# Conditioned attention on one core: a new order of the columns, with x, residual and output moved for pairs of steps, and all weights turned by VectorE

## The chip, the cores and the metric

The kernel runs on one core of one Trainium2 chip. The metric is device time in microseconds; lower is better. A change of the time is told from no change by runs of both kernels on the same chip.

## The reference

x is (8, 512, 512) in float32: 8 batches of 512 tokens of 512 columns. There are 16 heads of 32 columns.

```python
Q = split_heads(x @ Wq.T + bq);  K = split_heads(x @ Wk.T + bk);  V = split_heads(x @ Wv.T + bv)
tQ = split_heads(tokens @ Wq.T + bq);  tK = split_heads(tokens @ Wk.T + bk)   # one token per batch
cQ = Q + tQ;  cK = K + tK
scores = einsum('bhqd,bhkd->bhqk', cQ, cK) / sqrt(32)
attn = softmax(scores, axis=-1)
out = einsum('bhqk,bhkd->bhqd', attn, V)
x = x + out.transpose(0, 2, 1, 3).reshape(B, S, 512)
```

All is float32, and the weights are dense 512 x 512 matrices. The condition (`tokens`, 8 x 512) adds the same vector to each query and key of a batch.

## The kernel before

The work is cut into T = 32 steps: 8 batches times G = 4 groups of 4 heads. A step t holds the four heads of group t % 4 of batch t // 4, one head on each quarter of the 128 partitions. The order of the instructions on TensorE, VectorE, ScalarE and GpSimd is that in which the Python code records them; SyncE's transfers are put in an order by the framework, by when their operands are ready.

*Two kinds of steps.* The exponentials of a softmax must lie with the keys on the partitions for the product with V, but the row maxima are found with the queries there. Odd steps (`BLOCKED`) compute the scores once (`row_max`, L592; `row_scores`, L619), take the row maxima on VectorE (L588 and L630), and write the exponentials (`denominators`, L653) into the first eight rooms of `arena`. From there they are turned: SyncE moves blocks of 32 rows between partition quarters (`exchange`, L643, in two halves of 16 transfers of 128 KB), and VectorE turns each 32 x 32 block in place (`turn_blocks`, L636, eight turnings of 128 x 1024 for each odd step). Even steps compute the scores twice: once with the queries on the partitions, for the maxima and sums (their exponentials go back into PSUM), and once with the keys there (`exponentials`, L718), with the maxima brought in by a small matmul of `maxT` (L723). `maxT` is made by GpSimd (`split_max`, L675) and a transposing transfer on SyncE (`turn_max`, L692). These exponentials go to `arena` from room 8 on, eight rooms in a step, wrapping at `ROOMS`.

*The loop* runs over t = 1 to 28. Each step has four items:

- V: `weighted(t - 1)`, the product of step t - 1's exponentials with V (`times_v`, L739), then reciprocal, transpose, scaling, residual (`send`, L807),
- q, k, v: the projections of a later group, in the seven-product form of a 2 x 2 block product; four products in one step, three in the next (`four_products` L511, `three_products` L533).

Each item also holds the scores and maxima of one quarter of the queries of step t + 1 (or of t + 2, in the last item), their exponentials, and, in even steps, one quarter of `exponentials(t, i)`. The eight PSUM banks go round: `begin` (L133) deals four of them to the scores of an item. Which turnings follow which item is a table (`TURNED`, L1028: with u the odd step whose blocks are turned, (-1, 2) is the k item of step u - 1, and (0, 3) the v item of step u). Which transfers are recorded behind which item is a table too (`ORDERS`, L1040).

*The single buffer of blocks.* `room` (L222) has one buffer, so the exchange of the next odd step starts when `weighted` of the last one has read it, in the V item of the even step.

*Columns.* Group g is columns 128 g to 128 g + 127. `spread` (L161) gives 32 columns of every 32nd token, so that a transfer of x, of the residual (`load_residual`, L180) or of the output (`store`, L817) writes 32 partitions in 512 runs of 128 bytes, and four transfers make a step's tile; VectorE's block transpose (L373, L810) then turns it.

*The start* (L247 to L950). Wq by rows in four transfers, x of batch 0 and the first rows of Wk by rows, turned by TensorE and copied out of PSUM; the rest of Wk, and Wv, in runs of 128 bytes, turned by VectorE (`turn_w`, L900). `condition` and `condition_end` (L836, L844) compute the projected tokens. GpSimd makes the sums of weight blocks for the seven-product form (`combine_w`, L332; four sums for each weight).

Of the kernel before, what the change touches and what calls it, by code (L numbers as in the profile page):

```python
# [17 lines left out]
def kernel(  # L18
# [52 lines left out]
    ROOMS = 14  # L71
# [4 lines left out]
    xp = ctx.enter_context(tc.tile_pool(name="xp", bufs=2))  # L76
# [73 lines left out]
    xs = {}  # L150

    def load_x(n, queue=nc.sync):

        if n < B * NS:
            xs[n] = early[:, 3 + n, :]
            queue.dma_start(xs[n], x[n // NS, n % NS * P : (n % NS + 1) * P, :])

# [3 lines left out]
    def spread(a, d):  # L161

        return a.rearrange("(f j) d -> j f d", j=BL)[:, :, d : d + BL]

    def load_block(n):

        b, cc = divmod(n, NC)
        if b < B:
            xs[n] = xp.tile([P, NB, BL], F32, tag="x", name=f"x_{n}")
            for h in range(HG):  # L170
                nc.sync.dma_start(xs[n][h * BL : (h + 1) * BL], spread(x[b], cc * P + h * BL))

    xr = {}
    late = []
# [5 lines left out]
    def load_residual(t):  # L180

        b, g = divmod(t, G)
        if turned_by_vector(t):
            if late:
                xr[t] = late_part(t % 2 * 10 + 2).rearrange("p (f e) -> p f e", e=BL)
            else:
                xr[t] = op.tile([P, NB, BL], F32, tag="xr", name=f"xr_{t}", bufs=1)
            for h in range(HG):
                nc.sync.dma_start(
                    xr[t][h * BL : (h + 1) * BL], spread(x[b], g * P + h * BL)  # L190
                )
        else:

            xr[t] = xT[b][:, g, :]
# [32 lines left out]
    for n in ("q", "k", "v"):  # L227
        ws[n] = stage.tile([P, NC, D], F32, tag="w", name=f"w_{n}")

    def load_w(n, w, queue, cs=range(NC)):  # L230
        wv = w.rearrange("(c p) d -> p c d", p=P)
        for c in cs:
            queue.dma_start(ws[n][:, c, :], wv[:, c, :])
# [12 lines left out]

    load_w("q", Wq, nc.sync, [0])  # L247
    load_x(0, nc.scalar)
    load_x(1)
    wk0 = early[:, 7, :]  # L250
    nc.scalar.dma_start(wk0, Wk[:P, :])

    cond_sb = early[: B + 2, 0, :]
    nc.sync.dma_start(cond_sb[:B, :], cond)
    nc.sync.dma_start(cond_sb[B : B + 1, :], bq.rearrange("(o d) -> o d", o=1))
    nc.sync.dma_start(cond_sb[B + 1 : B + 2, :], bk.rearrange("(o d) -> o d", o=1))
    load_x(2)
    load_x(3, nc.scalar)
    load_w("q", Wq, nc.sync, [1])
    onesb = const.tile([P, P], BF16, tag="onesb", name="onesb")  # L260
    nc.vector.memset(onesb, 1.0)
    ones = const.tile([P, P], F32, tag="ones", name="ones")
    nc.vector.memset(ones, 1.0)
    table = const.tile([P, 1], F32, tag="table", name="table")
    nc.scalar.activation(table, ones[:, :1], AF.Exp)
    load_w("q", Wq, nc.sync, [2, 3])

    for n, w, f in (("k", Wk, HG), ("v", Wv, 0)):
        wn = ws[n].rearrange("p c (f e) -> p c f e", e=BL)
        for cc in range(NC):  # L270
            for h in range(HG):
                nc.sync.dma_start(
                    wn[h * BL : (h + 1) * BL, cc, f:], spread(w, cc * P + h * BL)[:, f:]
                )
    bvl = const.tile([P, 1], F32, tag="bvl", name="bvl")
    nc.sync.dma_start(bvl, bv.rearrange("(g p o) -> g p o", g=G, o=1)[G - 1])
    bvs = const.tile([P, G, BL], F32, tag="bvs", name="bvs")
    for h in range(HG):
        nc.sync.dma_start(
            bvs[h * BL : (h + 1) * BL],  # L280
            bv.rearrange("(o g h e) -> o h g e", o=1, g=G, h=HG)[:, h].broadcast_to([BL, G, BL]),
        )

# [14 lines left out]
    condT = const.tile([P, NC, HD], F32, tag="condT", name="condT")  # L298
    nc.vector.memset(condT, 0.0)
# [10 lines left out]
    def transpose_w(n, dc, pt, odd=None, of=None):  # L310

        odd = dc % 2 if odd is None else odd
        of = ws[n][:, dc, :] if of is None else of
        for cc in range(NC):
            nc.tensor.transpose(
                pt[:, cc * P : (cc + 1) * P], of[:, cc * P : (cc + 1) * P], ident
            )
        o = wT[n][:, :, dc * P : (dc + 1) * P]
        pv = pt.rearrange("p (c s) -> p c s", c=NC)
        if n == "q":  # L320
            if odd:
                nc.vector.tensor_scalar(o, pv, SCALE, None, ALU.mult)
            else:
                nc.scalar.activation(o, pv, AF.Copy, scale=SCALE)
        elif odd:
            nc.vector.tensor_copy(o, pv)
        else:
            nc.scalar.copy(o, pv)
# [23 lines left out]
    def transpose_x(n, pt, leaves=nc.vector.tensor_copy):  # L352

        b, sc = divmod(n, NS)
        if b >= B:
            return
        if sc == 0:
            xT[b] = xtp.tile([P, NC, S], F32, tag="xT", name=f"xT_{b}")
        for cc in range(NC):
            nc.tensor.transpose(  # L360
                pt[:, cc * P : (cc + 1) * P], xs[n][:, cc * P : (cc + 1) * P], ident
            )
        leaves(xT[b][:, :, sc * P : (sc + 1) * P], pt.rearrange("p (c s) -> p c s", c=NC))
        if n > 1:
            load_block(n + 2)

    def turn_x(n):
        b, cc = divmod(n, NC)
        if b >= B:
            return  # L370
        if cc == 0:
            xT[b] = xtp.tile([P, NC, S], F32, tag="xT", name=f"xT_{b}")
        nc.vector.transpose(xT[b][:, cc, :], xs[n].rearrange("p f i -> p (f i)"))  # L373
        to_load.append(n + 2)
# [3 lines left out]
    def load_blocks():  # L378
        while to_load:
            load_block(to_load.pop(0))  # L380
# [385 lines left out]
    def masked(t):  # L766
# [3 lines left out]
        apart = op.tile([P, HG, NS, NS], F32, tag="apart", name=f"apart_{t}")  # L770
# [36 lines left out]
    def send(t, y_, rec):  # L807
# [4 lines left out]
        nc.gpsimd.tensor_tensor(y, y, xr.pop(t), ALU.add)  # L812
        to_store.append((t, y))
# [3 lines left out]
    def store():  # L817
        while to_store:
            t, y = to_store.pop(0)
            b, g = divmod(t, G)  # L820
            for h in range(HG):
                nc.sync.dma_start(spread(out[b], g * P + h * BL), y[h * BL : (h + 1) * BL])
# [11 lines left out]
    part = {}  # L834

    def condition(n, pt):  # L836


        for cc in range(NC):
            nc.tensor.matmul(pt[cc * HD : (cc + 1) * HD, :], condT[:, cc, :], wT[n][:, cc, :])  # L840
        part[n] = early[:, 1 + "qk".index(n), :]
        nc.scalar.copy(part[n], pt)

    def condition_end(n, pt, on):  # L844

        i = "qk".index(n)
        untranspose(part[n], pt)
        sum4 = const.tile([P, NC, B], F32, tag=f"sum4{n}", name=f"sum4_{n}")
        nc.vector.tensor_reduce(
            sum4,  # L850
            pt.rearrange("p (d c e) -> p d e c", d=NC, c=NC)[:, :, 0:B, :],
            AX.X,
            ALU.add,
        )
        on.tensor_tensor(
            tok[:, i], sum4, bias2[:, i, :].unsqueeze(2).broadcast_to([P, NC, B]), ALU.add
        )
        on.tensor_tensor(apart_tok[:, i], tok[:, i, 1::2], tok[:, i, 0::2], ALU.subtract)
# [10 lines left out]
    def first_part(n, pt, h):  # L869
        for cc in range(NC):  # L870
            project_qk_part(0, n, cc, pt, slice(h * HS, (h + 1) * HS))

    transpose_w("q", 0, bank(6), 0)
    transpose_x(0, bank(3))
    transpose_x(1, bank(7), nc.scalar.copy)
    transpose_w("k", 0, bank(5), 1, wk0)
    pc = bank(1)
    BB = B + 2
    for cc in range(NC):
        nc.tensor.transpose(  # L880
            pc[:, cc * BB : (cc + 1) * BB], cond_sb[:, cc * P : (cc + 1) * P], ident[:BB, :BB]
        )
    pcv = pc[:, : NC * BB].rearrange("p (c b) -> p c b", b=BB)
    nc.vector.tensor_copy(condT[:, :, 0:B], pcv[:, :, 0:B])
    bias2 = const.tile([P, 2, NC], F32, tag="bias2", name="bias2")
    nc.vector.tensor_scalar(bias2[:, 0, :], pcv[:, :, B], 2.0 * SCALE, None, ALU.mult)
    nc.vector.tensor_scalar(bias2[:, 1, :], pcv[:, :, B + 1], 2.0, None, ALU.mult)
    first_part("q", pq, 0)
    transpose_x(2, bank(0))
    transpose_x(3, bank(3), nc.scalar.copy)  # L890
    first_part("k", pk, 0)
    for half in range(2):
        combine_x(0, half, nc.gpsimd)
    transpose_w("q", 1, bank(7), 1)
    first_part("q", pq, 1)
    transpose_w("q", 2, bank(1), 0)
    transpose_w("q", 3, bank(0), 1)
    first_part("k", pk, 1)

    def turn_w(n, ccs, rows=slice(0, D)):  # L900
        for cc in ccs:
            nc.vector.transpose(wT[n][:, cc, rows], ws[n][:, cc, rows])

# [421 lines left out]
```

## Time and profile before

| | |
|---|---|
| time, median of 3 runs | 712.62 us (711.2 to 715.9) |
| profiled execution: time | 712.44 us |
| profiled execution: span | 710.6 us |
| TensorE busy | 691.2 us (97%) |
| VectorE busy | 571.3 us (80%) |
| ScalarE busy | 544.6 us (77%) |
| GpSimd busy | 280.3 us (39%) |
| mean granted TensorE clock | 0.981 |
| DMA | 90.24 MB, 237273 packets, 221163 of them under 512 bytes |

A row of a view by time has the start, the length, the engine (PE is TensorE, DVE VectorE, ACT ScalarE, POOL GpSimd, SPq the issuing of transfers on SyncE), the line of the code, the operation, output <- input, the shape and a count; in brackets the idle time before it and what ended it. A row of the view by windows has the window and its length, then for PE, PEld (weight loads), DVE, ACT and POOL the busy time and the number of instructions, then the granted TensorE clock, the share of the DMA engines and GB/s. A row of the view by groups has the busy time, the mean length in ns, the idle time before and what ended most of it. A busy TensorE is not one at its peak: matmuls are pipelined, and a matmul that runs at a lower clock is busy for longer.

### The profile page before, as it was taken

How to read it: one execution, taken by the hardware profiler on the slowest of the kernel's cores; microseconds unless marked ns; L12 is line 12 of the kernel's file. 1: busy time of each engine (PE TensorE's matmuls, PEld its weight loads, DVE VectorE, ACT ScalarE, POOL GpSimd, SP SyncE). 2: the span in 40 equal slices, each digit the busy share in tenths (PEclk: the TensorE clock that was granted, in tenths of full speed). 3: DMA queues.
4: the chain of work that ended last, by engine and by line, in shares of the span. 5: the costliest groups of instructions: out<-in, count | busy, mean ns of one | idle time of the engine just before them, and what ended most of it. 6: DMA issues, size and time to landing. Idle time of an engine off the chain costs nothing.

```text
span 710.6 us, 21535 instructions
## 1 busy us (share of the span) xinstructions
PE 691.2 (97%) x8488; PEld 305.1 (43%) x8488; DVE 571.3 (80%) x810; ACT 544.6 (77%) x1399; POOL 280.3 (39%) x330
## 2 busy tenths in 40 slices
PE   9999999999999999999999999898999999999997
PEld 7444443444434444444434444343343444444432
DVE  3797887879688887969879787787878889697777
ACT  2587795978869798797968779687696978879664
POOL 3720532526236161444415254252542526243271
PEclk9999999999999999999999999999899999999999
DMA  6627548476776857677675766857577575663211
GB/s 183 105 39 167 121 108 177 81 157 139 154 153 115 182 94 164 140 152 161 121 160 105 149 142 124 175 97 159 121 141 164 103 168 120 142 150 51 34 31 30
DMA packets 237273, 90.24 MB, mean 127 GB/s; under 512 B 221163, under 2 KB 221675, under 8 KB 237173
## 3 DMA queue, kind: packets, MB, share of 16 engines
q1 hardware_dynamic: 235412, 87.83, 60.8%
q8 instruction: 66, 1.08, 0.7%
q10 hardware_dynamic: 1760, 1.05, 0.5%
q14 instruction: 35, 0.28, 0.1%
HBM read 19.75 MB, written 8.39 MB: 40 GB/s over the span
## 4 chain that ended last, share of the span: by engine, by line
PE 67%; SPq 16%; DMA 5%; DVE 4%; ACT 3%; issue 3%; POOL 0%; DVEq 0%; ACTq 0%; POOLq 0%
PE psum L463 27%; SPq L651 16%; PE psum L746 15%; PE psum L621 15%; PE psum L726 4%; DMA out_dram<-res 2%; PE psum L406 2%; ACT psum L667 2%; PE psum L723 2%; DVE nmax L588 2%; DMA blocks<-arena 1%; DVE blocks L641 1%; DVE nmax L630 1%; ACT arena L667 1%; DMA early<-in_x_dram 1%
## 5 line engine op out<-in xcount | busy, mean ns | idle before, releaser
L667 ACT ACTIVATE psum<-psum,nmax 128x512 f32<-128x512 f32 x256 | 169.0, 662 | 91.1 <-DVE nmax L588 79.8
L588 DVE TENSOR_REDUCE nmax<-psum 128x1 f32<-128x512 f32 x272 | 172.2, 678 | 43.0 <-PE psum L621 42.5
L621 PE MATMUL psum<-kT,qT 32*128 32x512 f32 x1024 | 177.1, 625 | 10.9 <-ACT psum L667 10.9
L641 DVE STREAM_TRANSPOSE blocks<-blocks 128x1024 f32<-128x1024 f32 x112 | 134.5, 1221 | 40.0 <-DMA out_dram<-res 24.8
L737 ACT ACTIVATE arena<-psum 128x512 f32<-128x512 f32 x264 | 136.4, 602 | 33.7 <-PE psum L726 24.5
L667 ACT ACTIVATE arena<-psum,nmax 128x512 f32<-128x512 f32 x224 | 152.8, 697 | 5.3 <-issue 4.9
L630 DVE TENSOR_REDUCE nmax<-psum 128x2 f32<-128x1024 f32 x114 | 138.1, 1212 | 1.1 <-PE psum L621 1.1
L202 POOL TENSOR_TENSOR xr<-xr,bvs 128x512 f32<-128x512 f32 x29 | 37.2, 1283 | 172.7 <-DMA xr<-in_x_dram 172.6
L621 PEld LDWEIGHTS psum<-kT,qT 32*128 32x128 f32 x1024 | 64.0, 183 | 89.5 <-ACT psum L667 33.1
L811 POOL TENSOR_TENSOR res<-res,recs 128x512 f32<-128x512 f32 x30 | 31.5, 1051 | 120.3 <-DVE res L810 111.0
L746 PE MATMUL psum<-arena,v 128*32 128x512 f32 x576 | 77.8, 659 | 0.0
L726 PE MATMUL psum<-qT,kT 32*128 32x512 f32 x528 | 67.9, 587 | 0.0
L746 PE MATMUL psum<-blocks,v 128*32 128x512 f32 x448 | 51.9, 596 | 0.0
L667 ACT ACTIVATION_READ_ACCUMULATOR psum<-psum,nmax 128x1 f32 x256 | 51.8, 202 | 0.0
L463 PE MATMUL psum<-wc_v,xc 128*32 128x256 f32 x768 | 50.6, 381 | 0.0
L463 PE MATMUL psum<-xc,wc_q 128*32 128x256 f32 x720 | 48.3, 387 | 0.0
L667 ACT ACTIVATION_READ_ACCUMULATOR arena<-psum,nmax 128x1 f32 x224 | 47.8, 213 | 0.0
L463 PE MATMUL psum<-xc,wc_k 128*32 128x256 f32 x720 | 47.4, 381 | 0.0
L810 DVE STREAM_TRANSPOSE res<-psum 128x512 f32<-128x512 f32 x28 | 19.5, 697 | 30.0 <-PE psum L746 30.0
L812 POOL TENSOR_TENSOR res<-res,xr 128x512 f32<-128x512 f32 x29 | 37.2, 1283 | 2.3
L463 PE MATMUL psum<-wT_v,xT 128*32 128x256 f32 x512 | 34.3, 382 | 0.2 <-ACT arena L737 0.2
L746 PEld LDWEIGHTS psum<-arena,v 128*32 128x32 f32 x576 | 15.9, 118 | 42.8 <-issue 23.5
(193 smaller groups left out, 894.2 us busy)
## 6 DMA issues: line engine op xcount, KB each, us to landing
blocks<-arena SPq DMA_DIRECT2D x448, 128.0 KB, 2.4
out_dram<-res SPq DMA_DIRECT2D x122, 64.0 KB, 2.1
xr<-in_x_dram SPq DMA_DIRECT2D x116, 64.0 KB, 2.4
x<-in_x_dram SPq DMA_DIRECT2D x112, 64.0 KB, 2.4
w_q<-in_L_cond_Wq_dram SPq DMA_DIRECT2D x4, 256.0 KB, 3.8
w_v<-in_L_cond_Wv_dram SPq DMA_DIRECT2D x16, 64.0 KB, 2.3
w_k<-in_L_cond_Wk_dram SPq DMA_DIRECT2D x16, 48.0 KB, 2.7
early<-in_x_dram ACTq DMA_DIRECT2D x2, 256.0 KB, 3.9
```

The costliest lines, as they stand in the source:

```text
L202: nc.gpsimd.tensor_tensor(xr[t], xr[t], bias, ALU.add)
L463: nc.tensor.matmul(pt[r], still[:, r], moving, start=(kc == kcs[0]), stop=(kc == kcs[-1]))
L588: nc.vector.tensor_reduce(nmax[t][:, qc, j : j + 1, 0], pt, AX.X, ALU.max, negate=True)
L621: nc.tensor.matmul(pt, qkT["q", t][r, qc * P : (qc + 1) * P], qkT["k", t][r, :], start=True, stop=True,)
L630: nc.vector.tensor_reduce(nmax[t][:, qc, pr * 2 : pr * 2 + 2, 0], pt, AX.X, ALU.max, negate=True)
L641: nc.vector.transpose(e, e)
L651: nc.sync.dma_start(to.rearrange("p c h s -> p (c h s)"), of)
L667: nc.scalar.activation(to, of, AF.Exp, bias=nmax[t][:, qc, j, :], accum_out=sums[t][:, qc, j, :],)
L726: nc.tensor.matmul(bank[j], qkT["k", t][r, kc * P : (kc + 1) * P], qkT["q", t][r, :], start=False, stop=True,)
L737: nc.scalar.activation(e[:, i, :], bank[pr * 2 + i], AF.Exp)
L746: nc.tensor.matmul(pt[j * HD : (j + 1) * HD, :], vs[b % 2][:, kc, (g * HG + j) * HD : (g * HG + j + 1) * HD], e, start=(kc == chunks[0]), ...
L812: nc.gpsimd.tensor_tensor(y, y, xr.pop(t), ALU.add)
```

## The change

- *Columns.* Group g now holds columns 32 g to 32 g + 31 of each quarter of the 512. Two steps that follow each other (g and g + 1) then lie side by side, and one transfer takes both in runs of 256 bytes: x (`load_pair`), the residual (`load_residual`, two pairs of buffers, loaded a pair ahead) and the output (`store`, once in a pair; GpSimd adds into the residual's tile, from where it is stored). The last four steps are stored one by one, and the last one in four transfers.
- *Weights.* All three come by rows in runs of 512 bytes (`load_rows`, `load_all`), Wq and Wk group by group, Wk's groups 1 to 3 issued from ScalarE; ScalarE scales Wq (`scale_rows`), and VectorE turns every block of weights and of x (`turn_w`, `turn_x`). TensorE's transposes at the start are gone. The projected tokens come from small matmuls with the token as the moving operand.
- *Turnings* of the exchanged blocks are dealt anew among the items.
- *Orders.* Output and x are recorded in the odd step's q item, the residual in its k item; nothing stands between the halves of the exchange.
- *Room.* `ROOMS` is 13, x has one buffer (of a pair), small constants lie in columns of the turned weights that are no longer read; `begin` sorts the two banks that it deals first.

```diff
-    ROOMS = 14
+    ROOMS = 13
...
-        order[w : w + 4] = [j for j in rows if j not in last] + list(last)
+        order[w : w + 4] = sorted(j for j in rows if j not in last) + list(last)
...
+    def load_pair(n):
+        b, k = divmod(n, NC // 2)
         if b < B:
-            xs[n] = xp.tile([P, NB, BL], F32, tag="x", name=f"x_{n}")
-            for h in range(HG):
-                nc.sync.dma_start(xs[n][h * BL : (h + 1) * BL], spread(x[b], cc * P + h * BL))
+            xs[n] = xp.tile([P, NB, 2, BL], F32, tag="x", name=f"x_{n}")
             for h in range(HG):
                 nc.sync.dma_start(
+                    xs[n][h * BL : (h + 1) * BL].rearrange("p f c e -> p f (c e)"),
+                    spread(x[b], h * P + k * 2 * BL, 2),
                 )
...
+            two = op.tile([P, NB, 2, BL], F32, tag="xr", name=f"xr_{t}", bufs=2)
+            twos[t // 2] = two
+            for h in range(HG):
+                nc.sync.dma_start(
+                    two[h * BL : (h + 1) * BL].rearrange("p f c e -> p f (c e)"),
+                    spread(x[b], h * P + g * BL, 2),
+                )
...
+    def load_rows(n, a, g, queues):
+        for h in range(HG):
+            queues[h].dma_start(
+                ws[n].rearrange("p (k g) c e -> p g k (c e)", g=G)[h * BL : (h + 1) * BL, g],
+                a.rearrange("(k g j) d -> g j k d", g=G, j=BL)[g, :, :, h * P : (h + 1) * P],
+            )
...
+    load_rows("q", Wq, 0, two_queues)
+    load_all(x0, x[0], two_queues)
+    load_rows("k", Wk, 0, two_queues)
...
+    scale_rows(0)
+    for g in range(1, G):
+        load_rows("q", Wq, g, [nc.sync] * HG)
+        load_rows("k", Wk, g, [nc.scalar] * HG)
+    load_all(ws["v"], Wv, [nc.sync] * HG)
...
+    def turn_w(n, g):
+        nc.vector.transpose(
+            wT[n][:, :, g * P : (g + 1) * P].rearrange("p c (h e) -> p c h e", h=HG),
+            ws[n].rearrange("p (h g) c e -> p g c h e", g=G)[:, g],
+        )
...
-        nc.gpsimd.tensor_tensor(y, y, xr.pop(t), ALU.add)
-        to_store.append((t, y))
+        nc.gpsimd.tensor_tensor(xr[t], y, xr[t], ALU.add)
+        if t % 2 or t >= T - 4:
+            to_store.append(t)
...
+    turn_w("q", 0)
     for cc in range(NC):
+        turn_x(cc)
+    project(0, "q", pq)
+    turn_w("k", 0)
...
+    condition("q", [0], bank(6))
+    condition("k", [0], bank(5))
     project_qk_end(0, "q", pq)
+    project(0, "k", pk)
     project_qk_end(0, "k", pk)
+    scale_rows(1)
+    turn_w("q", 1)
+    turn_w("k", 1)
...
-    TURNED = {(-1, 2): 1, (-1, 3): 1, (0, 0): 1, (0, 1): 1, (0, 2): 2, (0, 3): 2}
-    turned = {1: 2}
-    turn_blocks(1, range(2))
+    TURNED = {(-1, 3): 1, (0, 0): 1, (0, 1): 2, (0, 2): 1, (0, 3): 3}
+    turned = {1: 1}
+    turn_blocks(1, range(1))
...
-        (1, 1): ["store"],
-        (1, 2): ["residual", "x"],
+        (1, 1): ["store", "x"],
+        (1, 2): ["residual"],
...
-        (0, 2): ["store", "residual", 1],
+        (0, 2): [1],
...
-                    load_residual(t)
+                    if t + 3 <= T - 4:
+                        load_residual(t + 3)
```

More of the change, by code (lines that the diff above doesn't have):

```diff
@@ L308 @@
     }
[L310 to L328, printed above, removed]
+    def turn_w(n, g):
+        nc.vector.transpose(
+            wT[n][:, :, g * P : (g + 1) * P].rearrange("p c (h e) -> p c h e", h=HG),
+            ws[n].rearrange("p (h g) c e -> p g c h e", g=G)[:, g],
+        )
     wc = {}
```

272 lines of the change are left out of this document (126 added, 146 removed).

## Prediction

> **What bounds the kernel now.** I read the page first, then the windows by pair of steps, then one late pair engine by engine.
>
> ```profile
> PE 691.2 (97%) x8488; PEld 305.1 (43%) x8488; DVE 571.3 (80%) x810; ACT 544.6 (77%) x1399; POOL 280.3 (39%) x330
> PE 67%; SPq 16%; DMA 5%; DVE 4%; ACT 3%; issue 3%; POOL 0%; DVEq 0%; ACTq 0%; POOLq 0%
> ```
>
> TensorE looks full, yet a sixth of the chain that ended last lies in SyncE's queue, which computes nothing. The loop runs over 14 pairs (an odd step, whose exponentials go through the exchange, and an even one). I cut the span at the pairs:
>
> ```profile
> 75.40:120.40 45.00, 44.51 (x532) 19.06 (x536) 35.11 (x49) 34.90 (x91) 17.27 (x21) 0.92 0.60 127
> 120.40:162.00 41.60, 41.17 (x534) 18.04 (x533) 34.81 (x49) 33.53 (x88) 17.15 (x21) 1.00 0.65 130
> 162.00:205.40 43.40, 42.94 (x535) 18.42 (x531) 35.04 (x49) 34.42 (x91) 17.18 (x21) 0.96 0.72 148
> 587.70:628.70 41.00, 40.54 (x536) 17.95 (x534) 33.68 (x47) 34.06 (x90) 17.16 (x21) 1.00 0.65 138
> ```
>
> The same matmuls take 41.0 us in a good pair and 43 to 45 us where the granted clock (third column from the end) fell below 1. Now the good pair, SyncE, VectorE, ScalarE, TensorE in turn:
>
> ```profile
> 606.82 10.40 SPq L651 DMA_DIRECT2D blocks<-arena  x16
> 617.34 2.20 SPq L822 DMA_DIRECT2D out_dram<-res  x4
> 619.58 2.10 SPq L189 DMA_DIRECT2D xr<-in_x_dram  x4
> ...
> 616.85 0.41 DVE L544 TENSOR_TENSOR kT<-psum,kT 128x256 f32<-128x256 f32 x1
> 619.48 1.25 DVE L641 STREAM_TRANSPOSE blocks<-blocks 128x1024 f32<-128x1024 f32 x1 [2.22 <-DMA out_dram<-res]
> 620.65 1.25 DVE L588 TENSOR_REDUCE nmax<-psum 128x1 f32<-128x512 f32 x2
> ...
> 621.39 0.66 ACT L667 ACTIVATE psum<-psum,nmax 128x512 f32<-128x512 f32 x1 [1.46 <-DVE nmax L588]
> ...
> 617.62 1.03 PE L621 MATMUL psum<-kT,qT 32*128 32x512 f32 x8
> ...
> 621.31 1.12 PE L621 MATMUL psum<-kT,qT 32*128 32x512 f32 x2
> 622.89 1.13 PE L621 MATMUL psum<-kT,qT 32*128 32x512 f32 x6 [0.46 <-ACT psum L667]
> 623.96 1.06 PE L746 MATMUL psum<-arena,v 128*32 128x512 f32 x8
> ...
> 627.59 1.14 PE L621 MATMUL psum<-kT,qT 32*128 32x512 f32 x8
> ...
> 632.25 1.14 PE L621 MATMUL psum<-kT,qT 32*128 32x512 f32 x8
> 633.32 1.07 PE L463 MATMUL psum<-xT,wT_k 128*32 128x256 f32 x16
> ```
>
> The 16 transfers of the exchange's first half cannot be issued before 606.82 (the buffer is read until then), and issue takes 10.40 us. VectorE is done with kT at 617.26 and next in its order is the first turning of these blocks: it stands 2.22 us until the last transfer lands. (The row names an output store, but that queue's stores were issued behind the blocks; the wait is for the blocks.) The row maxima behind it start late, then the exponentials, then the scores, whose bank is freed late: scores that need 1.07 us from start to next (632.25 to 633.32) take 2.65 us (621.31 to 623.96). So even the best pair loses 1.58 us. In a worse one the gap also costs clock:
>
> ```profile
> 71.58 1.13 PE L621 MATMUL psum<-kT,qT 32*128 32x512 f32 x4
> 73.60 1.79 PE L621 MATMUL psum<-kT,qT 32*128 32x512 f32 x4 [0.89 <-ACT psum L667]
> 75.33 1.26 PE L463 MATMUL psum<-xT,wT_q 128*32 128x256 f32 x16
> 76.33 1.95 PE L463 MATMUL psum<-xc,wc_q 128*32 128x256 f32 x16
> ...
> 628.66 1.07 PE L463 MATMUL psum<-xT,wT_q 128*32 128x256 f32 x16
> ```
>
> Here the scores took 3.75 us, and the next products 1.95 us instead of about 1.05. The rows at 75.33 and 628.66 are the same instruction in the first and the last pair, 13 periods apart: 553.3/13 = 42.56 us a pair.
>
> **The change part by part.** *Turnings dealt anew.* The first of the eight turnings of a step moves from the even step's k item to its v item, behind the three sums of v; two stand in the odd step's q, one in k, three in v. This is the edit that pays. In the pair above the first turning would come due after the v sums. Without the wait the maxima start about 1.05 us behind their scores (617.62), at 618.7, and take 2.4 us (four sums of 128x512 at about 0.6); the sums end with v's last product, which the scores at 621.31 follow, near 622.4. The blocks landed by 619.48: the wait of 2.22 us goes, and 2.9 us of slack stand there. What is late next? I go through the odd step with the group rows:
>
> ```profile
> L588 DVE TENSOR_REDUCE nmax<-psum 128x1 f32<-128x512 f32 x18 | 11.4, 678 | 3.6 <-PE psum L621 3.6
> L641 DVE STREAM_TRANSPOSE blocks<-blocks 128x1024 f32<-128x1024 f32 x9 | 10.8, 1218 | 2.2 <-DMA out_dram<-res 2.2
> L630 DVE TENSOR_REDUCE nmax<-psum 128x2 f32<-128x1024 f32 x7 | 8.5, 1211 | 0.0
> ```
>
> Per item the maxima take 2.4 us; V has reciprocal and transpose besides (0.9). With turnings of 1.2: V 4.5, q 4.8, k 3.6, v 6.0, in all 18.9 us; TensorE's pace is four items of 4.66 (the scores of q and k, 627.59 to 632.25), 18.6. VectorE is then level with TensorE over the odd step and recovers in the even one, where it waits several times a microsecond (the 3.6 us of the first row). I allow 0.1 us a pair for it. *Cover:* the last three turnings end just before the product that reads them; if they slip, TensorE stands for the slip.
>
> *Pairs in 256-byte runs.* Per pair of steps x, residual and output take 12 transfers instead of 24, of 128 KB each. Before, eight of 64 KB:
>
> ```profile
> 586.59 1.14 PE L621 MATMUL psum<-kT,qT 32*128 32x512 f32 x8
> 559.06 4.20 SPq L171 DMA_DIRECT2D x<-in_x_dram  x8
> 596.62 1.22 SPq L697 DMA_TRANSPOSE wT_v<-split  x1
> 641.58 0.39 PE L723 MATMUL psum<-wT_v,onesb 3*128 3x512 bf16 x4
> 612.71 2.06 ACT L737 ACTIVATE arena<-psum 128x512 f32<-128x512 f32 x4
> blocks<-arena SPq DMA_DIRECT2D x448, 128.0 KB, 2.4
> DMA to landing us min/median/max: 2.4/2.5/4.5
> ```
>
> (The last row is the transpose's own, L697.) The eight take 0.525 us each, with 512 runs. Doubled runs cost between 0.525 (by runs) and 1.05 (by bytes); the exchange moves 128 KB in 10.40/16 = 0.65, so I take 0.6: 7.2 us instead of 12.6. Where they stand counts more: the built order of SyncE is exchange (32 without a break), output 4, x and residual 8, turning of the maxima (L697 before), exchange. Nothing stands between the halves any more, and the second half's turnings come 4 us after their landing. The loads now stand ahead of the transpose of the maxima: exchange 606.82 + 20.8 = 627.6, loads to 634.8, and the transpose becomes ready where it did, 10.0 us behind the odd step's q scores (596.62 against 586.59, the same instruction a pair earlier), so at 627.59 − 1.58 + 10.0 = 636.0. Cover 1.2 us, and the transpose lands 1.5 us before TensorE reads it (636.0 + 2.5, against 641.58 − 1.58); priced at 0. The residual is loaded a pair ahead, so GpSimd's long waits for it go, but they held nothing.
>
> *13 rooms instead of 14.* The third item's second pair of exponentials now writes a room that the exchange reads with its first four transfers. These are issued by 609.4 and land by 611.8; the write is the third activation of the row at 612.71, near 613.7. Free by 1.9 us. *Banks sorted*, *sums kept in spare weight columns*, output added in place: no instruction more on any engine of the loop; 0.
>
> *The start.* All weights come by rows and VectorE turns 12 blocks and 4 of x; TensorE's transposes go.
>
> ```profile
> 6.23 9.78 SPq L272 DMA_DIRECT2D w_k<-in_L_cond_Wk_dram  x16
> 21.64 0.70 DVE L902 STREAM_TRANSPOSE wT_v<-w_v 128x512 f32<-128x512 f32 x1
> 23.04 1.14 PE L621 MATMUL psum<-kT,qT 32*128 32x512 f32 x8
> 32.37 1.28 POOL L344 TENSOR_TENSOR wc_v<-wT_v 128x512 f32<-128x512 f32 x1
> 40.81 0.27 POOL L684 TENSOR_TENSOR split<-rest,split 128x16 bf16<-128x16 f32 x1
> ```
>
> ScalarE issues 12 transfers of Wk ahead of kT: at 9.78/16 = 0.61 each, from about 8.5, to 16; scores then start near 17, not 23.04. But from there VectorE has, up to the last turning of v, ten turnings of 0.70, three rounds of maxima (7.3) and about 4.5 of sums: 19 us, to 36, or 39 with waits on TensorE. GpSimd then combines v (four of 1.28) ahead of the split of the first maxima, which ends at 42.3 to 45.3 instead of 41.08. I take +3 us; bounds −3 (the earlier scores carry through) and +9 (loads or turnings twice as slow in part).
>
> The Trainium skill, "TensorE: Matmul & The Clock Gate", Part 1, says that after about 3.4 us of idleness the array's clock is halved until as much busy time has passed. This trace agrees on the halving (1.95 for about 1.05), though after a gap of only 0.89. By that rule the first projections after the warm-up matmuls would run at half speed, an estimate of 2 us more at the start, and the sum below would be 675.
>
> *The end:* the last output goes out in four transfers of short runs instead of two: +0.5.
>
> **Sum.** The profiled execution took 712.4 us (span 710.6), beside a median of 712.6. A pair becomes 41.0 − 1.58 + 0.1 = 39.5, without the clock losses: 13 × (42.56 − 39.5) = −39.8. The first pair's late scores: 3.75 − 1.07 = −2.7. Start +3, end +0.5. 712.4 − 39.8 − 2.7 + 3 + 0.5 = 673.4; I say 674.
>
> **The rivals.** *Another wait takes the place* (0.17): seven turnings in the odd step, or the transpose of the maxima, keep a pair at the 41.0 of the best one. For: both have only tenths to spare. Against: TensorE bears maxima up to a microsecond late in the odd step, as it does now. 712.4 − 13 × 1.56 − 2.7 + 3.5 = 693.
>
> *The exchange is as late as before* (0.05): it can't start until the old blocks are read, and if its landing slips 3 us, all stays: 42.56 a pair, 712.4 + 3.5 = 716. Against: nothing new stands ahead of it.
>
> *Slower: the doubled transfers cost by bytes* (0.08). At 1.05 each the 12 end at 640.2, the transpose lands 2.5 to 4.5 later, while the even step needs it at 640.0 (641.58 less the 1.58 gained): 3.5 us of standing, and 1.7 of clock (43.40 against 41.60 in the windows). 39.5 + 5.2 = 44.7 a pair, 712.4 + 28 − 2.7 + 3.5 = 741. It decides from about 0.94 us a transfer. Against: 128 KB of exchange took 0.65.
>
> The Trainium skill, "DMA: Bandwidth & Descriptors", section Specifications, asks for runs of 512 bytes for line rate, so that 256 still falls short; it gives no price for them here, and no run so far shows one.
>
> **How the numbers follow.** Forecast 0.70, rivals 0.17, 0.05, 0.08. Low end 664: start −3 and 39.2 a pair (712.4 − 43.7 − 2.7 − 3 = 663). High end 696: the first rival with 3 us more at the start. Faster by over 1% 0.87, within 1% 0.05, slower 0.08; 1% is about what a measurement of this kernel tells from no change.
>
> **What would show it.** Right: pairs of 39 to 40 us at clock 1.00, no idle time on VectorE before the first turning, odd-step scores at 1.07 us, 12 transfers a pair near 0.6 us. Wrong: waits of the L723 matmuls for the transposed maxima, VectorE without pause through the odd step and TensorE standing, or the split of the first maxima after 50 us.

## The result, and the profile after

The changed kernel takes 707.45 us (median of 20 runs, 701.3 to 714.5) beside 712.77 us (20 runs, 707.0 to 718.3) for the kernel before: a ratio of 0.9912, 95% interval 0.9887 to 0.9937. Ratios, here and below, are taken over the fast runs alone: eight of the 20 runs of the changed kernel are over 1.5% longer than its fastest and count as slow, and the median of the other twelve is 705.8 us. The change makes the kernel faster, but by 0.6 to 1.1%, where 5.4% was forecast; the time lies 33 us above the forecast of 674 and above the range. Its profiled execution took 703.8 us, span 702.0.

First the page of the changed kernel: the engines, and the chain that ended last.

```profile
PE 667.4 (95%) x8472; PEld 298.3 (42%) x8472; DVE 572.1 (81%) x814; ACT 542.0 (77%) x1397; POOL 279.5 (40%) x331
PE 78%; DMA 9%; SPq 4%; POOL 3%; ACT 3%; DVE 2%; issue 1%; ACTq 0%; DVEq 0%; POOLq 0%
```

SyncE's queue has gone from 16% of the chain to 4%: what bounded the kernel before is mended. In its place stand 9% of landing transfers and 3% of GpSimd. TensorE is busy for 24 us less (in part because fewer matmuls run at a low clock), yet the span fell by 8.6 only.

Where the time lies is seen when the span is cut at the start of the q products in the first and in the last odd step. Between the two cuts lie 13 pairs of steps, the loop. Windows of the kernel before (three rows), then of the changed one (three rows):

```profile
0.00:75.30 75.30, 72.88 (x768) 38.62 (x768) 54.68 (x101) 43.48 (x110) 23.63 (x31) 1.00 0.61 126
75.30:628.70 553.40, 542.60 (x6869) 235.52 (x6870) 453.00 (x624) 442.98 (x1158) 223.56 (x261) 0.98 0.68 139
628.70:710.60 81.90, 75.71 (x860) 30.93 (x856) 63.64 (x87) 58.12 (x133) 33.15 (x40) 0.98 0.27 50
...
0.00:90.40 90.40, 78.82 (x756) 40.27 (x758) 55.38 (x105) 42.84 (x109) 23.65 (x32) 0.92 0.49 112
90.40:619.20 528.80, 512.82 (x6872) 226.82 (x6868) 452.27 (x623) 441.31 (x1157) 222.79 (x261) 0.99 0.64 144
619.20:702.00 82.80, 75.71 (x860) 31.26 (x856) 64.45 (x88) 57.89 (x133) 33.08 (x40) 0.98 0.23 47
```

| us | before | forecast | after |
|---|---|---|---|
| up to the first odd step's q products | 75.3 | 75.6 (−2.7 + 3) | 90.4 |
| 13 pairs | 553.4 | 513.6 (−39.8) | 528.8 |
| the rest | 81.9 | 82.4 (+0.5) | 82.8 |

So the miss of 30.4 us (703.8 against 673.4) has two halves: 15.2 in the loop, 14.8 at the start. In the loop TensorE's busy time is near the 513.6 us that the forecast gave the whole loop, 512.8; 16 us of standing lie on top.

*The loop.* Two pairs that follow each other, and VectorE's turnings and the small matmuls of the maxima by groups:

```profile
130.00:169.40 39.40, 39.40 (x536) 17.54 (x533) 34.79 (x49) 33.83 (x90) 17.18 (x21) 1.00 0.64 148
169.40:211.40 42.00, 39.47 (x536) 17.38 (x536) 34.82 (x49) 34.17 (x91) 17.13 (x21) 1.00 0.67 148
...
L627 DVE STREAM_TRANSPOSE blocks<-blocks 128x1024 f32<-128x1024 f32 x112 | 133.0, 1217 | 0.0
L709 PE MATMUL psum<-wT_v,onesb 3*128 3x512 bf16 x264 | 26.6, 388 | 16.0 <-DMA wT_v<-split 15.0 <-ACT v L510 1.0
```

The wait ahead of the first turning is gone (0.0 us over all 112 turnings), and a pair without a wait takes 39.4 us at full clock. But the second pair holds the same 39.5 us of work in 42.00. The missing 2.53 is one wait, and the last group says for what: the transposed maxima, now 15.0 us in all, where it was 0.2 in the kernel before. SyncE's queue (issue) in the clean pair and in the late one, and TensorE where it reads them in the late one:

```profile
131.75 2.27 SPq L813 DMA_DIRECT2D out_dram<-xr  x4
134.12 0.48 SPq L165 DMA_DIRECT2D x<-in_x_dram  x1
135.91 2.22 SPq L192 DMA_DIRECT2D xr<-in_x_dram  x4
138.17 1.55 SPq L165 DMA_DIRECT2D x<-in_x_dram  x3
139.82 1.23 SPq L683 DMA_TRANSPOSE wT_v<-split  x1
149.12 22.70 SPq L637 DMA_DIRECT2D blocks<-arena  x32
171.92 3.26 SPq L813 DMA_DIRECT2D out_dram<-xr  x4
175.28 0.47 SPq L165 DMA_DIRECT2D x<-in_x_dram  x1
176.92 1.91 SPq L192 DMA_DIRECT2D xr<-in_x_dram  x4
178.88 1.54 SPq L165 DMA_DIRECT2D x<-in_x_dram  x3
180.53 1.23 SPq L683 DMA_TRANSPOSE wT_v<-split  x1
...
184.88 0.40 PE L709 MATMUL psum<-wT_v,onesb 3*128 3x512 bf16 x4 [2.53 <-DMA wT_v<-split]
```

The rows follow each other in the order of the queue. Between x and the residual it stands still for 1.2 to 1.3 us (175.75 to 176.92): the residual goes into the tile from which the output has just been sent, so its load waits until the output has landed. SyncE's own waits name this: 14.5 us in 15 waits of the residual's load for an output. The transpose stands behind all of it. In the late pair it is issued 11.2 us behind the pair's start (9.9 in the clean one), and TensorE reads its result 4.35 us after that issue; in the clean pair 3.05 were enough. A pair without a wait reads it 12.9 us behind its start. Over the 13 pairs the issue lies at 9.1 to 13.0, and nine of them stand for 0.4 to 3.3 us; in the worst, of 45.17 us, TensorE stands for 3.26 and the granted clock over the pair is 0.92.

*The start.* TensorE, with one turning of Wq on VectorE, GpSimd's last part of the split, and the first exchange on SyncE:

```profile
9.68 5.53 PE L392 MATMUL psum<-xT,wT_q 128*128 128x512 f32 x8 [5.46 <-DVE xT L358]
16.75 3.68 PE L392 MATMUL psum<-xT,wT_k 128*128 128x512 f32 x8
21.20 1.14 PE L607 MATMUL psum<-kT,qT 32*128 32x512 f32 x8 [0.78 <-ACT kT L407]
21.70 0.71 DVE L324 STREAM_TRANSPOSE wT_q<-w_q 128x512 f32<-128x512 f32 x1 [3.95 <-ACT w_q L286]
23.38 5.38 PE L392 MATMUL psum<-xT,wT_q 128*128 128x512 f32 x8
34.09 1.95 PE L836 MATMUL psum<-early,wT_q 128*128 128x8 f32 x16
35.89 2.30 PE L836 MATMUL psum<-early,wT_k 128*128 128x8 f32 x16
38.12 1.94 PE L449 MATMUL psum<-xT,wT_q 128*32 128x256 f32 x16
55.52 0.27 POOL L670 TENSOR_TENSOR split<-rest,split 128x16 bf16<-128x16 f32 x1
55.84 0.61 PE L693 MATMUL psum<-identb,split 128*128 128x128 bf16 x4 [3.14 <-POOL split L670]
70.99 20.34 SPq L637 DMA_DIRECT2D blocks<-arena  x27
```

The first scores start at 21.20, before at 23.04, but nothing of that lasts. The same eight matmuls take 5.53, 3.68 and 5.38 us. In the last of these the granted clock shows why: it is 0.50 from 24 to 25. In the first, behind 5.46 us without work, the record of the clock reads 1.00, so the profile alone does not show the cause; experiment 6 shows that the loss goes when TensorE is kept busy. VectorE waits 3.95 us for ScalarE's scaling of Wq's second group, which stands behind kT. The projected tokens cost 64 matmuls with 8 moving columns each, by the trace's count (here the last 32, 4.25 us). The granted clock is 1.00 when these 32 begin and 0.50 from 38 to 40, and the products behind them take 1.94 us where 1.07 is usual. The split of the first maxima ends at 55.79 (before 41.08); TensorE stands for it, and the clock is 0.50 from 55 to 61. (The last row, the first exchange, is cut off where its view ends, at 91.)

### The profile page after: what moved, and what is told of

It is laid out like the page before. It is cut to its first block, busy times and chain, and to the rows that moved or that the text cites. A ratio compares the mean times of both kernels' runs of the same rounds, so it can differ in the third digit from the quotient of the medians.

```text
span 702.0 us, 21260 instructions
## 1 busy us (share of the span) xinstructions
PE 667.4 (95%) x8472; PEld 298.3 (42%) x8472; DVE 572.1 (81%) x814; ACT 542.0 (77%) x1397; POOL 279.5 (40%) x331
## 4 chain that ended last, share of the span: by engine, by line
PE 78%; DMA 9%; SPq 4%; POOL 3%; ACT 3%; DVE 2%; issue 1%; ACTq 0%; DVEq 0%; POOLq 0%
PE psum L449 31%; PE psum L732 16%; PE psum L607 16%; PE psum L712 8%; DMA wT_v<-split 4%; PE psum L709 3%; SPq L637 2%; DMA out_dram<-xr 1%; PE psum L392 1%; DMA early<-in_x_dram 1%; DMA xr<-in_x_dram 1%; SPq L813 1%; PE psum L836 1%; ACT arena L653 1%; DMA w_q<-in_L_cond_Wq_dram 1%
## 5 line engine op out<-in xcount | busy, mean ns | idle before, releaser
L607 PE MATMUL psum<-kT,qT 32*128 32x512 f32 x1024 | 153.9, 623 | 0.8 <-ACT kT L407 0.8
L627 DVE STREAM_TRANSPOSE blocks<-blocks 128x1024 f32<-128x1024 f32 x112 | 133.0, 1217 | 0.0
L607 PEld LDWEIGHTS psum<-kT,qT 32*128 32x128 f32 x1024 | 56.9, 184 | 64.1 <-issue 29.2
L732 PE MATMUL psum<-arena,v 128*32 128x512 f32 x576 | 69.4, 597 | 0.0
L653 ACT ACTIVATION_READ_ACCUMULATOR arena<-psum,nmax 128x1 f32 x224 | 49.7, 222 | 0.0
L709 PE MATMUL psum<-wT_v,onesb 3*128 3x512 bf16 x264 | 26.6, 388 | 16.0 <-DMA wT_v<-split 15.0
L800 POOL TENSOR_TENSOR xr<-res,xr 128x512 f32<-128x512 f32 x30 | 38.4, 1280 | 2.4
L205 POOL TENSOR_TENSOR xr<-xr,wT_q 128x512 f32<-128x512 f32 x30 | 38.1, 1271 | 0.0
L449 PEld LDWEIGHTS psum<-wc_v,xc 128*32 128x32 f32 x768 | 23.4, 110 | 25.7 <-ACT arena L723 10.6
```

Source lines behind the costliest of these rows:

```text
L205: nc.gpsimd.tensor_tensor(xr[t], xr[t], bias, ALU.add)
L449: nc.tensor.matmul(pt[r], still[:, r], moving, start=(kc == kcs[0]), stop=(kc == kcs[-1]))
L607: nc.tensor.matmul(pt, qkT["q", t][r, qc * P : (qc + 1) * P], qkT["k", t][r, :], start=True, stop=True,)
L627: nc.vector.transpose(e, e)
L653: nc.scalar.activation(to, of, AF.Exp, bias=nmax[t][:, qc, j, :], accum_out=sums[t][:, qc, j, :],)
L709: nc.tensor.matmul(bank[j], onesb[r, :], maxT[t][r, :], start=True, stop=False)
```

## The experiments

Each kernel is the changed one with the edit shown, except the first; the numbers are medians, and ratios to runs of the kernel before on the same chip, with their 95% intervals.

**1. The new turnings alone, in the kernel before.**

```diff
-    TURNED = {(-1, 2): 1, (-1, 3): 1, (0, 0): 1, (0, 1): 1, (0, 2): 2, (0, 3): 2}
-    turned = {1: 2}
-    turn_blocks(1, range(2))
+    TURNED = {(-1, 3): 1, (0, 0): 1, (0, 1): 2, (0, 2): 1, (0, 3): 3}
+    turned = {1: 1}
+    turn_blocks(1, range(1))
```

> The kernel before with the new dealing of the turnings alone (the table of turnings and the first one ahead of the loop); columns, transfers and start as before. Theory: the moved first turning is what pays in the loop. Then VectorE's wait before the first turning goes, a pair of steps takes 39.4 to 39.8 us instead of 42.56, and as the start keeps its 75.3 us and the transposed maxima keep their place ahead of the loads, the time is 712.4 - 13 x 2.9 - 2.7 = about 672 us. Rival: without the longer runs the second half of the exchange, issued behind eight short transfers, lands too late for its turnings, pairs stay at 41 or above and the time at 692 or above.

Measured: 692.17 us, ratio 0.9718 [0.9664, 0.9771]; 13 pairs in 533.9 us beside 553.4 (mean 41.07, best 39.43). From its waits:

```profile
DVE blocks L641 <- DMA blocks<-arena: 13.2, 6, 4.3
DVE blocks L641 <- DMA out_dram<-res: 12.5, 8, 2.4
PEld L723 <- DMA wT_v<-split: 11.8, 8, 2.2
```

The table of turnings alone gives 20 us, more than the whole change. It doesn't give the whole pair: the theory's 672 us is missed by 20, and what the rival named is what happened. With output and residual still between the halves of the exchange, the second half lands late and VectorE goes on waiting for blocks (25.7 us in all, in the first two rows), and the maxima come late too. The sign of the step is shown; its size needs the unbroken exchange as well.

**2. The old turnings, in the changed kernel** (the edit of 1 the other way round).

> The changed kernel with the old dealing of the turnings; all else as changed. Theory: the first turning waits again some 2 us for the exchange, pairs of 39.4 us vanish and none is below 40.9; the mean goes from 40.7 to about 42, the time from about 704 to about 720. Rival: the fewer and longer transfers had let the exchange land earlier, so that the old dealing finds its blocks too; pairs of 39.4 remain and the time is 700 to 708.

Measured: 722.54 us, ratio 1.0134 [1.009, 1.0177]; no pair under 41.0, 13 pairs in 549.6 us. The group of the turnings:

```profile
L627 DVE STREAM_TRANSPOSE blocks<-blocks 128x1024 f32<-128x1024 f32 x112 | 134.5, 1221 | 36.5 <-DMA blocks<-arena 36.5
```

The wait is back (0.0 to 36.5 us, 13 times) and costs 20.8 us of the loop. Shown from both sides: the turnings are the edit that pays, about 20 us in either kernel's loop.

**3. All three loads behind the transpose of the maxima.**

```diff
-        (1, 1): ["store", "x"],
-        (1, 2): ["residual"],
-        (1, 3): [],
+        (1, 1): [],
+        (1, 2): [],
+        (1, 3): ["store", "x", "residual"],
```

> The changed kernel with output, x and residual recorded in the odd step's last item, so that SyncE issues the transpose of the maxima ahead of them. Theory: the maxima are late because their transpose stands in SyncE's queue behind the loads, one of which waits for the output's landing. Then the idle time of TensorE before the L709 matmuls (36 us) falls below 3, all pairs take 39.4 to 39.7 us, and the profiled span falls by 13 x 1.2 = 15 us to about 687. Rival: the transpose itself lands late (4.3 instead of 2.5 us) under the traffic of the memory, wherever it stands: the waits remain, pairs at 40.7 in the mean, span 700 to 704. A second rival: the loads now push the exchange back by more than its slack of 2 to 3 us, ScalarE waits for the rooms and VectorE for the blocks, and pairs take 41 or more.

Measured: 710.33 us, ratio 0.9988 [0.9949, 1.0028]; 13 pairs in 535.9 us. From the waits:

```profile
DVE xT L358 <- DMA blocks<-arena: 14.0, 7, 2.9
DVE xT L358 <- DMA x<-in_x_dram: 5.8, 4, 2.4
PEld L709 <- DMA wT_v<-split: 2.4, 3, 1.1
```

Half right. The waits for the maxima are gone (21.1 to 2.4 us), so the place in the queue is their cause; but now x, which VectorE turns in the next V item, lands too late (both first rows are waits of that turning, which reads x alone; the first row names the exchange, which that turning does not read). One wait was traded for another.

**4. Of the loads, only the residual behind the transpose** (and x recorded ahead of the output).

```diff
-        (1, 1): ["store", "x"],
-        (1, 2): ["residual"],
-        (1, 3): [],
+        (1, 1): ["x", "store"],
+        (1, 2): [],
+        (1, 3): ["residual"],
```

> The changed kernel with another order of the transfers in a pair: x and output behind the exchange, as now, then the transpose of the maxima, and only the residual moved behind it. Theory (the residual's load waits in SyncE's queue for the output's landing, and the transpose behind it is issued late and lands in 4.3 us among other transfers): the waits for the transposed maxima (21.1 us of weight loads and 15.0 of matmuls) fall below 6 in all, x is still in time, pairs 39.4 to 40.0 beside 40.68, 13 pairs 9 to 16 us shorter, time 691 to 698. Rival (VectorE level with TensorE in the odd step, or the exchange, keeps the mean pair at 40.5 or more whatever stands ahead of the transpose, as with all three loads moved behind it): time 705 to 709.

Measured: 687.9 us, ratio 0.9663 [0.9583, 0.9743]. All 13 pairs take 39.41 to 39.77, 513.0 us together (528.8 before the edit). SyncE in a pair that starts at 169.5, and the wait that is left:

```profile
172.11 3.25 SPq L165 DMA_DIRECT2D x<-in_x_dram  x4
175.46 2.14 SPq L813 DMA_DIRECT2D out_dram<-xr  x4
178.57 1.21 SPq L683 DMA_TRANSPOSE wT_v<-split  x1
179.97 2.94 SPq L192 DMA_DIRECT2D xr<-in_x_dram  x4
...
PEld L709 <- DMA wT_v<-split: 2.4, 4, 0.9
```

The transpose is issued 9.1 us behind the pair's start in each of the 13, as soon as the split is there, instead of 9.1 to 13.0; the residual's load, now behind it, no longer waits for an output at all (14.5 us before the edit). The loop gets back 15.8 us, all of the 15.2 that it lay above the forecast and a little more. VectorE, level with TensorE on paper, holds nothing. Whether putting x ahead of the output matters by itself was not run.

**5. The first maxima split ahead of the sums of Wv, on GpSimd.** `combine_w("v")` is recorded behind `split_max(0)` instead of before it.

> The changed kernel with the sums of Wv's blocks on GpSimd recorded behind the split of the first maxima instead of ahead of it. Theory: at the start TensorE stands 3.1 us for the split and then runs at half clock for 5 us because GpSimd first makes the four sums of Wv. Then the first odd step's q products start 4 to 6 us earlier (90.4 to about 85.5) and the span falls by as much, to about 697. Rival: the delay sits in the chain before (VectorE's turnings and TensorE's cold clock), and the sums of Wv become the next wait in front of the first product of v: under 1.5 us gained.

Measured: 704.18 us, ratio 0.9851 [0.9782, 0.992]. In its profiled run (709.43 us, the longest of the four) the split ends at 53.5 instead of 55.8, but the first odd step's q products start only 1.8 us earlier (88.6): ScalarE's copy of the transposed maxima goes into a part of wT_v that those same sums read, so it waits 3.65 us for GpSimd all the same. Mostly a miss: what stood between was not the order of two things but that both are late.

**6. TensorE kept warm: 110 warm-up matmuls instead of 28.**

> The changed kernel with 110 instead of 28 warm-up matmuls, so that TensorE is busy until x of batch 0 is turned; nothing else. Theory (a cold clock is part of the late start): the first projections (L392, 8 matmuls) take about 2.6 us instead of 5.53, the second set 1.9 instead of 3.68, and the first odd step's q products start 3 to 5 us before 90.4, at 85.5 to 87.5; time 702 to 704.5. Rival (loads, VectorE's turnings and GpSimd's sums set the start, the clock is hidden): the first projections are shorter but the first odd step's q products stay within 1.5 us of 90.4, time 706 to 708.

Measured: 699.29 us, ratio 0.9842 [0.9748, 0.9935]; the first odd step's q products at 87.0.

```profile
9.27 3.67 PE L392 MATMUL psum<-xT,wT_q 128*128 128x512 f32 x8
21.12 3.68 PE L392 MATMUL psum<-xT,wT_q 128*128 128x512 f32 x8
```

5.53 and 5.38 became 3.67 and 3.68, and 3.4 us of it arrive at the loop. (The expectation's 2.6 and 1.9 for these matmuls were wrong: 3.7 us is their time at full clock, as it was in the kernel before.) Clock is part of the late start, under a quarter of it. Its runs go from 696.2 to 706.7 and those of the changed kernel from 701.3 to 714.5, so the medians don't size these 3.4 us; the position in the trace does. The reason is the loop: with the maxima still late, its 13 pairs take 528.8 us in the changed kernel's profiled run, 535.1 here, 536.2 in experiment 5 and 523.4 in 7, though none of these edits touches it. What moves them from run to run stays open.

**7. Another order at the start**, on ScalarE, VectorE and GpSimd: Wq's second group is scaled ahead of kT, and Wv is turned and combined right behind Wk.

```diff
+    scale_rows(1)
     project_qk_end(0, "k", pk)
-    scale_rows(1)
...
     combine_w("k")
+    for g in range(G):
+        turn_w("v", g)
+    combine_w("v")
     load_pair(2)
...
-    turn_w("v", 0)
-    turn_w("v", 1)
...
-    turn_w("v", 2)
-    turn_w("v", 3)
-    combine_w("v")
```

> The changed kernel with another order at the start alone: ScalarE scales Wq's second group ahead of kT, VectorE turns all of Wv behind the last group of Wk, and GpSimd combines Wv right behind Wk instead of ahead of the split of the first maxima. Theory (GpSimd's and VectorE's order set the 55.8 at which the split of the first maxima ends): the split ends at 45 to 50, the first odd step's q products start at 82 to 87 instead of 90.4, time 699 to 704. Rival (TensorE's own chain at a cold clock, with the small products of the condition, sets it): the split ends earlier, but the first odd step's q products start within 2 us of 90.4, time 705.5 to 708.

Measured: 698.27 us, ratio 0.9796 [0.9718, 0.9873]; the first odd step's q products at 84.8.

```profile
52.19 0.27 POOL L670 TENSOR_TENSOR split<-rest,split 128x16 bf16<-128x16 f32 x1
53.01 0.40 PE L693 MATMUL psum<-identb,split 128*128 128x128 bf16 x4
```

The split ends at 52.46, later than expected (45 to 50), for it now waits for the maxima themselves; but TensorE no longer stands for it (3.14 us before), nor loses clock behind it. This gives 5.6 us at the loop's start, over a third of what was lost; the three moves were not run apart.

**8. Edits 4, 6 and 7 together**, run twice.

> The three edits together: 110 warm-up matmuls, the start's new order, the residual behind the transpose of the maxima. If the three causes are apart from each other, their gains add up: the first odd step's q products start at 78 to 82, pairs 39.4 to 40.0, time 680 to 688, below both kernels and below the new turnings alone (692.2). If the start's causes hide each other, 688 to 694. If the late maxima are not what holds the pairs, 698 or more.

> The three edits together once more, as the measure for the run beside it: 677 to 681.

Measured: 679.08 and 678.94 us, ratios 0.9532 [0.9463, 0.9602] and 0.9532 [0.9501, 0.9562]. The q products start at 81.4 and 82.0 (8.4 to 9.0 us earlier; 3.4 + 5.6 = 9.0 from the two edits), pairs 39.41 to 39.59. The gains add up, so the three causes do not hide each other.

**9. The last 32 small matmuls of the projected tokens in the form of the kernel before**: the token stationary, matmuls of 256 columns on quarters of the array (eight by the trace's count for each weight), a copy, two transposes and a sum.

> The three edits together, and the projected tokens of the last two groups made as in the kernel before: the token is the stationary operand (4 matmuls of 256 columns on quarters of the array for each weight, a copy on ScalarE, two transposes) instead of 32 matmuls with 8 moving columns (1.95 and 2.02 us), which leave the next products at half clock (1.94 and 1.76 us for 1.07). Theory (these small matmuls and the clock behind them are what is left of the late start): the products behind them take 1.07, the first odd step's q products start 2.5 to 4.5 us before 81.4, time 2 to 5 us below the run beside it. Rival (GpSimd's sums, wc_q ready at 31.8, or the copy on ScalarE hold the products instead): they start where they did, within 1 us, and the times agree within 1 us.

> The kernel of the run before it once more, as the measure for the run beside it: 675 to 678, the first odd step's q products near 80.1.

Measured: 676.36 and 675.75 us, ratios 0.951 [0.9484, 0.9537] and 0.9438 [0.9398, 0.9477]; the run of 8 beside the first of them took 678.94. TensorE at the place, then further on, where it stands, with ScalarE and SyncE:

```profile
30.43 0.61 PE L857 MATMUL psum<-wT_k,early 128*32 128x256 f32 x8
31.96 1.07 PE L449 MATMUL psum<-xT,wT_q 128*32 128x256 f32 x16
...
66.48 1.49 PE L449 MATMUL psum<-wc_v,xc 128*32 128x256 f32 x16 [3.17 <-ACT v L487]
...
65.08 1.08 ACT L723 ACTIVATE arena<-psum 128x512 f32<-128x512 f32 x2 [3.81 <-DMA blocks<-arena]
...
57.69 22.66 SPq L637 DMA_DIRECT2D blocks<-arena  x32
```

The products behind the small matmuls run at full clock (1.07 for 1.94), and the transposed maxima of step 0 are taken at 44.85, 3.8 and 4.9 us earlier than in the two runs of 8. Of this 1.3 to 3.2 us arrive at the loop (80.1 and 78.8). The rest stops at a new place: ScalarE must not write the room that the first exchange still reads, and that exchange is late.

**10. The third pair of x no longer loaded ahead of the first exchange**, on top of 9: one `load_pairs()` is left out behind `turn_x(NC + 3)`, and the loop's own order loads the pair in the first odd step.

> That kernel with one load moved: the third pair of x is no longer loaded ahead of the first exchange but behind it, in the first odd step's q item. In the run before, the four transfers of this load waited for their buffer until 55.68 and the exchange behind them started at 57.69; ScalarE's exponentials then waited 3.81 us for the room that the exchange reads (there are 13 rooms), and TensorE 3.17 us behind them. Theory (the first exchange is late in SyncE's queue, and the room is read late): the exchange starts 1 to 3 us earlier, the waits fall by as much, the first odd step's q products start at 77.5 to 79, time 1 to 2.5 us below the run beside it. Rival (the exchange starts when its exponentials are written, whatever stands ahead): start at 57.5 or later and the times agree within 0.7 us.

Measured: 673.53 us (673.3 to 674.0) beside 675.75 for 9, ratio 0.941 [0.9375, 0.9446]. The exchange starts at 54.91 instead of 57.4 to 57.7, no room is late any more, and the loop starts 3.3 to 4.6 us earlier, where 1 to 3 were expected. The three windows of this kernel are:

```profile
0.00:75.50 75.50, 73.33 (x824) 39.66 (x824) 57.99 (x107) 43.47 (x111) 23.77 (x32) 1.00 0.59 130
75.50:588.30 512.80, 512.42 (x6868) 227.81 (x6864) 451.37 (x623) 440.97 (x1157) 222.84 (x261) 1.00 0.67 149
588.30:671.50 83.20, 75.61 (x860) 31.00 (x856) 64.70 (x88) 57.89 (x133) 33.17 (x40) 0.98 0.26 49
```

The start is back at the 75.3 us of the kernel before, and in 512.8 us of loop TensorE stands for 0.4. This version beats both kernels and the turnings alone.

## Why the prediction was right or wrong

*Turnings dealt anew: right.* VectorE's wait ahead of the first turning fell to 0.0, and a clean pair takes 39.4 us (39.5 forecast). Experiments 1 and 2 show that this edit carries it. The clock losses go with the waits: the mean granted clock is 0.981 before, 0.993 in experiment 1 and 0.976 in experiment 2.

*Transfers: right in size.* The twelve took 6.5 us of issue in the clean pair and 7.2 in the late one, for 7.2 forecast; x and residual cost 0.48 to 0.56 each. That refutes the slower rival, which began to decide at 0.94. The Trainium skill, "DMA: Bandwidth & Descriptors", Specifications, asks for 512-byte runs. What the step from 128 to 256 bytes shows here is that twice the bytes in as many runs took no longer to issue (0.525 before); they landed later, 2.8 and 2.9 us after issue in the median, 2.4 before.

*"Cover 1.2 us, and the transpose lands 1.5 us before TensorE reads it; priced at 0": this step failed in the loop.* Three of its numbers were off, all to the same side; their sizes here are those of the late pair shown. The exchange took 22.7 us of issue, not 20.8. The residual's load waits 1.2 us for the output to land, a wait the change itself brought in when it let the output be sent from the residual's tile, and which the step did not list. And the transpose, among other transfers, was read 4.35 us after its issue where 2.5 was taken for its landing. That is 1.9 + 1.2 + 1.8 = 4.9 us against 2.7 of cover: 2.2 us of standing, where 2.53 was measured. The term priced at 0 came to 16 us of standing over the 13 pairs, and put the loop 15.2 us above the forecast. The rival "another wait takes the place" named the transpose of the maxima and is what happened in the loop (40.68 a pair, 41.0 named). Experiment 4 takes the wait away by order alone, and the 13 pairs then take 513.0 us for 513.6 forecast. The prediction did not agree with itself here: its sum gave the transpose 2.7 us of cover, its rival "only tenths".

*The start, "+3, bounds −3 and +9": this term failed too.* It came to +15.1 beside before, or +17.8 with the 2.7 us that the late scores of the first pair were to give back. The path was the one described (GpSimd combines Wv ahead of the split), and the warning sign named, a split after 50 us, came true at 55.79. What was mis-sized: VectorE's chain was counted from scores at 17, as busy time with 3 us of waits, while it waited for ScalarE's scaling (3.95 us) and for TensorE. Three things were not in the sum. (a) Clock: 3.4 us by experiment 6. (b) The projected tokens as matmuls of 8 columns: 0.95 to 1.06 us for each group of a weight while the clock is full, and the clock behind them. (c) The first exchange behind two loads of x. Of the 14.9 us between 90.4 and 75.5, warm-up and order gave 8.4 to 9.0, then (b) 1.3 to 3.2 at the loop, and then (c) the rest, 3.3 to 4.6; (b) and (c) were run only on top of the edits ahead of them.

The estimate of 2 us that the prediction drew from the Trainium skill, "TensorE: Matmul & The Clock Gate", Part 1, was right for what it named: after 5.46 us of idleness the first projections took 5.53 us, and 3.67 when kept warm, 1.86 less. It was left out of the sum.

*13 rooms: right in the loop, wrong in the first pair.* "Free by 1.9 us" was worked out from a late pair. At the first exchange, which is behind loads, ScalarE waited for the room 2.54 to 3.81 us in experiment 9. In the changed kernel itself the slow start hid most of it.

*The end:* +0.9 for +0.5.

That the last experiment lands on 673.5 us, beside a forecast of 674, does not make the forecast right: it is this kernel with the five further edits of experiments 4, 6, 7, 9 and 10, and the agreement to half a microsecond is chance. What it shows is that these five account for both halves of the miss: its start of 75.5 us and its loop of 512.8 stand beside 75.6 and 513.6 forecast.

## What to carry to other kernels

When a wait is taken out of a loop, go through the in-order queue of the new program transfer by transfer: price what stands ahead of each transfer that an engine will soon read, and ask of every load whose last read or write of its buffer it waits for; a transfer whose data is needed late (here the residual, a pair ahead) belongs behind one whose data is needed now. Where loops are repaired, look at the first pass by itself: clock, order of three engines and the first use of a buffer are priced there once, but can eat as much as a loop gains. And run the edits of a change apart: here one table of turnings alone was worth three times the whole change.

## What the runs showed of the hardware

- Matmuls with 8 moving columns did not keep the clock up. During 32 of them in a row without idle time (4.0 and 4.6 us in 8, 4.25 in the changed kernel) the granted clock fell from 1.00 to 0.50, or did so right at their end, and the next products took 1.94 us. Where 16 wide ones and four transposes stood instead, the clock stayed at 1.00 and the same products took 1.07.
- The transposing transfer of the maxima landed 2.4 to 2.5 us after its issue in experiment 4, with the residual's load behind it, and 2.5 to 4.0 in the changed kernel, with all loads ahead of it. The order of the queue is not all: experiments 5 and 6 have the same order of transfers in the loop as the changed kernel, and there it landed after 2.5 to 2.6 and after 3.6 to 4.6; in one run of 8, ordered as in 4, up to 4.1.
